# Cross-attention by two levels of Strassen-Winograd products on one core: a fifth product in blocks, left sums by accumulating DMA

## The chip, the cores and the metric

The kernel runs on one core of a Trainium2 chip. The metric is the device time of one execution in microseconds (us); smaller is better. The profile comes from one further execution, with the hardware profiler on.

## What is computed

The reference, for each of 8 batches (C1 = C2 = 512, N = 1024, D = 64, all float32):

```python
q = einsum('bcn,dc->bnd', x1, Wq) + bq
k = einsum('bcn,dc->bdn', x2, Wk) + bk[:, None]
v = einsum('bcn,dc->bdn', x2, Wv) + bv[:, None]
attn = softmax(einsum('bnd,bdm->bnm', q, k), axis=2)
out = einsum('bcm,bnm->bcn', v, attn) + x1
```

The kernel never forms v. It multiplies the raw context by the exponentials first (y = x2 times e, with the contraction over the 1024 context positions m), scales y by the reciprocals of the sums of e, and then multiplies by Wv (o = Wv y), adding bv and x1 at the end.

## The kernel before

**Tiling and stages.** All eight batches run one after the other; `period(s, n, nn, nnn)` (L720) works on batch s and prepares the next ones (n, nn, nnn). The batch index `s.b` counts from 0, so `s.b == 2` is the third batch; the text below calls it batch 3. In a period the matrix engine (PE) runs, in this order:

- products 1, 2 and 6 of y, each a 256 x 512 result in two banks,
- the scores of the next batch for half 0 (the first 512 of the 1024 queries), then its following queries (`queries`, L158),
- products 5, 7 and 3 of y,
- the scores of the next batch for half 1, then keys (`keys`, L169),
- product 4 of y,
- the seven products of o (1, 6, 2, 5, 7, 3, 4).

**The two levels.** y is one 2 x 2 Strassen-Winograd product: left operands are the quarters "11", "12", "21", "22" of x2 transposed (`a`, L128) and their sums S1 to S4 (`left_sums`, L101), right operands are the exponentials `e` and their sums T1 to T4 (`right_sums`, L259). Seven products give four quarters of the result. A product is done either directly (`multiply`, L319: 2 x 4 matmuls of 512 columns) or once more by Strassen-Winograd, "in blocks" (7 x 2 matmuls of 256 columns). In blocks there are two forms. `multiply_seeded` (L415) opens new banks and copies its partial results into them on ScalarE (ACT). `multiply_onto` (L445) adds to open banks and copies partial results to a tile `d` in SBUF. Both run seven small products in the order 1, 7, 6, 2, 5, 4, 3. Small products 1, 6, 5 (and 4 in the seeded form) accumulate in one bank called chain, small product 7 in one called third, and an ACT copy takes each partial result out. A product in blocks needs its own sums, made on VectorE (DVE): `inner_left` (L373, four of 128x256) and `inner_right` (L382, four of 128x512).

Before the change products 1, 2, 3, 4 are in blocks from batch 3 on, product 7 in batches 3 to 6 and in the eighth (`seven`, L725), and products 5 and 6 are direct everywhere. Batch 1 has products 3 and 4 in blocks, batch 2 products 2, 3 and 4.

**Order.** The scheduler is switched off (`tc.manual_schedule()`, L948): each engine runs its instructions in the order in which the code issues them, and waits in place when an operand is not there. A dict of hooks hangs other ACT work between the copies of a product in blocks. The engines are PE, DVE, ACT, GpSimd (POOL, which issues accumulating DMAs and runs the all-reduces over partitions) and SyncE (SP, which issues loads and stores).

**PSUM.** Two banks a0, a1, two banks c0, c1, and a pool `ps_s` of two slots (tag "sc"), which scores, keys, queries, chain and third, and the two halves j of the first product of o (`multiply_o1`, L349) share. A new tile in that pool waits until the last reader of the slot is done.

**Names that the steps use.** `copy_first` (L569, ACT) copies tile 0 of the exponentials of half 0 to a running sum, and `add_tile` (L566, POOL) adds tiles 1 to 3 to it by accumulating DMAs of 512 KB, each of which waits for the landing of the one before. `total` (L223) sums over partitions. `shares` (L232) makes the reciprocals and spreads them over partitions by two small DMAs. `evict_y` (L499) adds a bank and a kept partial result, and scales by the reciprocals (`rden`). `sum_y` (L299) makes T1 to T4 of the second level, that of o. `evict_o` (L513) adds the bias, and adds x1 by an accumulating DMA. `load_x` (L122) issues four loads of 512 KB for the queries or keys of a coming batch, which wait until the last matmul that reads the single x tile is done.

Of the kernel before, what the change touches and what calls it, by code (L numbers as in the profile page):

```python
# [15 lines left out]
def kernel(  # L16
# [47 lines left out]
    nc = tc.nc  # L64
# [36 lines left out]
    def left_sums(a, *ks):  # L101

        for k in ks:
            x, y, op = {
                "S1": ("21", "22", ALU.add),
                "S2": ("11", "S1", ALU.subtract),
                "S3": ("11", "21", ALU.subtract),
                "S4": ("12", "S2", ALU.add),
            }[k]
            nc.vector.tensor_tensor(a["21" if k == "S3" else k], a[x], a[y], op)  # L110
            if k == "S3":
                a["S3"] = a["21"]
# [27 lines left out]

    def project(s, nm, w_sb, bank=None):
# [16 lines left out]
    def queries(s):  # L158

        ps = project(s, "q", wq_sb)  # L160
        s.q = sb.tile([P, N], F32, tag="q", name=f"q_{s.b}", bufs=2)
        for h, r, o in ((0, lo, hi), (1, hi, lo)):
            nc.scalar.activation(
                s.q[r, ts(h, H)], ps[r, :], AF.Identity, bias=bq_sb[r, :]
            )
        for h, r, o in ((0, lo, hi), (1, hi, lo)):
            nc.scalar.dma_start(s.q[o, ts(h, H)], s.q[r, ts(h, H)])
# [131 lines left out]
    def sum_y(s, k):  # L299
        if k == "T1":  # L300
            for n in ("T1", "T2", "T4"):
                s.y[n] = sb.tile([P, 2, H], F32, tag=f"y{n}", name=f"y{n}_{s.b}")
            s.y["T3"] = s.y["12"]
        right_sums(s.y, k)
# [44 lines left out]
    def multiply_o1(s):  # L349
# [16 lines left out]
    RIGHT = (  # L366
        ("T3", "22", "12", ALU.subtract),
        ("T1", "12", "11", ALU.subtract),
        ("T2", "T1", "22", ALU.subtract),
        ("T4", "21", "T2", ALU.add),  # L370
    )

# [9 lines left out]
    def inner_right(s, i, x, *tags):  # L382
# [4 lines left out]
        shape = [P, 4 // len(tags), MH // 2, H // 2]  # L387
        sums = [sb.tile(shape, F32, tag=t, name=f"eI{i}{t}_{s.b}") for t in tags]
        for z, (k, x, y, op) in enumerate(RIGHT):
            v[k] = sums[z // shape[1]][:, z % shape[1]]  # L390
            nc.vector.tensor_tensor(v[k], v[x], v[y], op)
        s.inner[i, "t"] = v
# [16 lines left out]
    def inner_parts(s, i):  # L409

        ks = ("third", "chain") if i in (2, 3) else ("chain", "third")
# [64 lines left out]
    def multiply_4(s):  # L476

        d, complete = multiply_onto(s, 4, "u5" if s.b < B - 1 else "a21", "r")
        complete()
        for j in range(2):  # L480
            u6 = s.tmp[6][:, j, :]
            nc.vector.tensor_tensor(u6, u6, d[:, j, :], ALU.add)

    def multiply_3(s, hooks):

        d, complete = multiply_onto(s, 3, "u1", "r", hooks)

        def evict():
            complete()
            s.y["12"] = y = sb.tile([P, 2, H], F32, tag="y12", name=f"y12_{s.b}")  # L490
            for j in (1, 0):
                nc.vector.tensor_tensor(y[:, j, :], s.bank["a", j], d[:, j, :], ALU.add)

        return evict

# [3 lines left out]
    def evict_y(s, k, steps=(1, 2)):  # L499

        bank, add = RESULT[k]
        rden = s.rden.get(int(k[1]) - 1)
        if 1 in steps:
            s.y[k] = sb.tile([P, 2, H], F32, tag=f"y{k}", name=f"y{k}_{s.b}")
        y = s.y[k]
        for step in steps:
            for j in range(2):
                if step == 1:
                    nc.vector.tensor_tensor(y[:, j, :], s.bank[bank, j], s.tmp[add][:, j, :], ALU.add)  # L509
                else:  # L510
                    nc.vector.tensor_tensor(y[:, j, :], y[:, j, :], rden, ALU.mult)  # L511
# [198 lines left out]
    def scores_and(n, h, bank, project):  # L710


        for i in range(MH):
            scores(n, h, i, bank if i == 2 else None)()
# [5 lines left out]
    def period(s, n, nn, nnn):  # L720

        late = s.b >= 2
        seven = late and (s.b < B - 2 or n is None)  # L725

        def first(i, hook=None):
            multiply(s, "y", i, s.a, s.t, MH, hook=hook)
# [7 lines left out]
        open_t(s)  # L736
        if n is None:
            load_x(s, x1)
        if late:
            complete_1 = multiply_seeded(s, 1, "y11")  # L740
        else:
            first(1)
        if s.b == 0:
            head_second(s, n)
        if late:
            shares(s, 0)
            sum_e(s, "T1", "T2", of=(0,))
            complete_1()
            sum_e(s, "T1", "T2", of=(2,))
            for i in range(1, MH):  # L750
                fold(s, 1, i, "sum", ALU.add)
            total(s, 1)
        else:
            sum_e(s, "T1", "T2")
            total(s, 0)
        if s.b == 0:
            load_a(n, "11")
            first(2)
            evict_y(s, "11", (1,))
            keys(n)  # L760
            load_x(nn, x1)
            sum_t4(s)
            sums(s, 1)
            shares(s, 0)
            sum_e(s, "T3")
        else:
            complete_2 = multiply_seeded(
                s,
                2,
                "y22",  # L770
                {5: lambda: copy_u1(s, 0), 4: lambda: copy_u1(s, 1)} if late else {},
            )
            if late and n:
                sum_t3(s, 0)
                sum_t3(s, 2)
            elif not late:
                sums(s, 1)
            complete_2()
            evict_y(s, "11", (1,))
            if s.b == 1:  # L780
                shares(s, 0)
            sum_t4(s)
            if not late:
                sum_a(s, "S4")
            if not late or n is None:
                sum_e(s, "T3")
        if s.b == 0:
            load_a(n, "21", "22")
        first(6)
        if s.b == 1:  # L790
            inner_right(s, 4, s.t["T4"], "eT2")
            inner_left(s, 3, s.a["S4"], "aI3")
        if seven:
            inner_left(s, 7, s.a["S3"], "yT4")
        if late:
            sum_a(s, "S4")
            inner_left(s, 4, s.a["22"], "a12")
            evict_y(s, "11", (2,))

        def add_exponential(i):  # L800
            exponential(n, 0, i)
            add_tile(n, 0, i)

        def next_queries():
            queries(nn)
# [7 lines left out]
        if n:  # L813
            scores_and(n, 0, "c", next_queries if nn else nothing)
            for i in range(1, MH):
                fold(n, 0, i, "max", ALU.max)
            highest(n, 0)
        if s.b == 0:
            inner_left(s, 4, s.a["22"], "a12")
            inner_right(s, 4, s.t["T4"], "eT2")  # L820
            inner_left(s, 3, s.a["S4"], "aI3")
        shares(s, 1)
        if seven:
            inner_right(s, 7, s.t["T3"], "yT1", "yT2")
            hooks = [{}, {}]
            if n:
                for i in range(MH):
                    lower(n, 0, i)
                hooks = [
                    {  # L830
                        1: lambda: copy_first(n, 0),
                        6: lambda: add_exponential(1),
                        5: lambda: add_exponential(2),
                    },
                    {6: lambda: add_exponential(3)},
                ]
# [146 lines left out]
```

## Time and profile before

| what | value |
|---|---|
| median of 3 runs | 686.92 us (686.87 to 687.68) |
| the profiled execution | 686.51 us |
| its span, first to last instruction | 684.7 us |
| outside the span | 1.8 us |
| PE busy | 677.9 us |
| DVE busy | 617.2 us |
| ACT busy | 303.6 us |
| POOL busy | 211.5 us |
| DMA share of batches 3 to 5 (window 204.20 to 453.10 us) | 0.74 to 0.75 |
| batch 4, first matmul of product 1 to that of batch 5 | 287.05 to 370.11 us |

How to read it: in the list of groups a row gives a line and engine, the operation, the tiles, a shape, a count, then busy time and the mean of one instruction, then the idle time of the engine ahead of them and what ended it. PE's matmuls appear twice per call (a float32 matmul of the code is two records), so a product of 8 matmuls is a row of 16. In a timeline a row is a run of equal instructions with its start and length; a number in brackets is the time that the engine sat idle before it, and after the arrow is what it waited for. "Issue to landing" of a DMA runs from the start of the issuing instruction to the completion that a waiter sees.

### The profile page before, as it was taken

Reading aid. Unit: us, or ns where it says so; the run is one execution under the profiler, and the core shown is the slowest. Engines: PE = TensorE matmul, PEld = TensorE weight load, DVE = VectorE, ACT = ScalarE, POOL = GpSimd, SP = SyncE. Lnnn points to the kernel's source line nnn. Section 1 sums busy time; section 2 is a strip of 40 time slices with the busy share of each in tenths; the row PEclk is TensorE's granted clock in tenths of the full one; section 3 lists DMA queues with packets and bytes.
Section 4 is the critical chain, followed back from the end, with each engine's and each line's share of the span. In section 5 each row is a group of like instructions: output and inputs, shape, how many; then the busy total and the mean of one; then the engine's idle time right before and its main releaser. Section 6 shows DMA issues by size and latency. Waiting matters only on the chain.

```text
span 684.7 us, 6896 instructions
## 1 busy us (share of the span) xinstructions
PE 677.9 (99%) x2324; PEld 378.3 (55%) x2324; DVE 617.2 (90%) x796; ACT 303.6 (44%) x500; POOL 211.5 (31%) x157
## 2 busy tenths in 40 slices
PE   9999999999999999999999999999999999999997
PEld 5333554535547465565656556464754745556763
DVE  1999998987999997999979998999989979999984
ACT  2734264236345552555524655426545355343220
POOL 0124112521333314243232512734227251424100
PEclk9999999999999999999999999999999999999999
DMA  9666365945747977569677696597942993368403
GB/s 304 264 220 222 81 232 103 219 124 137 246 86 176 188 181 245 102 159 219 177 219 149 138 258 137 194 178 159 247 91 81 224 188 71 70 116 232 114 9 114
DMA packets 46163, 114.28 MB, mean 167 GB/s; under 512 B 5041, under 2 KB 7345, under 8 KB 46129
## 3 DMA queue, kind: packets, MB, share of 16 engines
q0 software_dynamic: 18864, 41.50, 34.9%
q1 hardware_dynamic: 25856, 70.13, 29.5%
q10 hardware_dynamic: 1408, 2.23, 1.1%
q8 instruction: 18, 0.29, 0.2%
q14 instruction: 17, 0.13, 0.1%
HBM read 72.62 MB, written 16.81 MB: 131 GB/s over the span
## 4 chain that ended last, share of the span: by engine, by line
PE 94%; DMA 4%; SPq 1%; ACT 1%; DVE 1%; issue 0%; DVEq 0%
PE ps_ya L334 18%; PE ps_oa L334 12%; PE ps_oc L334 8%; PE ps_yc L398 8%; PE ps_s L191 6%; PE ps_ya L398 5%; PE ps_o L334 4%; PE ps_o L354 4%; PE ps_q L149 4%; PE ps_k L149 3%; PE ps_i4chain L398 3%; PE ps_i3chain L398 3%; PE ps_yc L334 3%; PE ps_i2chain L398 3%; PE ps_i1chain L398 2%; PE ps_i7chain L398 2%
## 5 line engine op out<-in xcount | busy, mean ns | idle before, releaser
L334 PE MATMUL ps_ya<-eT,aS 128*128 128x512 f32 x256 | 113.1, 595 | 0.0
L226 POOL PARTITION_ALL_REDUCE den<-sum x16 | 72.6, 4536 | 58.0 <-DVE sum L215 53.2
L334 PEld LDWEIGHTS ps_ya<-eT,aS 128*128 128x128 f32 x256 | 48.0, 190 | 60.9 <-issue 58.7
L253 ACT ACTIVATE e<-e 128x1024 f32<-128x1024 f32 x60 | 62.5, 1061 | 26.6 <-DVE e L249 25.6
L249 DVE TENSOR_TENSOR e<-e,top 128x1024 f32<-128x1024 f32 x60 | 69.3, 1214 | 3.7 <-POOL top L221 3.7
L221 POOL PARTITION_ALL_REDUCE top<-max x16 | 32.7, 2042 | 108.1 <-DVE max L215 54.7
L334 PE MATMUL ps_oa<-yT,w_S 128*128 128x512 f32 x128 | 57.6, 593 | 0.0
L200 ACT COPY e<-ps_s 128x1024 f32<-128x1024 f32 x46 | 45.7, 1027 | 19.1 <-PE ps_s L191 18.6
L345 ACT COPY uy<-ps_ya 128x512 f32<-128x512 f32 x36 | 21.0, 587 | 64.9 <-PE ps_ya L334 60.2
L191 PE MATMUL ps_s<-q,k 64*128 64x512 f32 x188 | 47.3, 608 | 0.8 <-ACT q L602 0.8
L567 POOL DMA_DIRECT2D sum<-e x21 | 25.8, 1228 | 66.3 <-DMA sum<-e 41.5
L334 PEld LDWEIGHTS ps_oa<-yT,w_S 128*128 128x128 f32 x128 | 24.2, 190 | 30.8 <-issue 29.7
L511 DVE TENSOR_TENSOR y<-y,den 128x512 f32<-128x512 f32 x64 | 40.3, 682 | 0.0
L211 DVE TENSOR_TENSOR max<-max,e 128x1024 f32<-128x1024 f32 x30 | 36.7, 1225 | 3.4 <-DVE max L211 0.5
L238 POOL DMA_DIRECT2D den<-row x16 | 9.0, 560 | 94.6 <-DMA row<-few 94.6
L563 POOL DMA_DIRECT2D uo<-in_x_dram x14 | 16.5, 1180 | 63.1 <-DVE few L234 36.8
L509 DVE TENSOR_TENSOR y<-ps_yc,uy 128x512 f32<-128x512 f32 x48 | 30.7, 679 | 0.0
L345 ACT COPY uo<-ps_oa 128x512 f32<-128x512 f32 x32 | 18.2, 588 | 28.0 <-PE ps_oa L334 28.0
L191 PEld LDWEIGHTS ps_s<-q,k 64*128 64x128 f32 x188 | 16.7, 186 | 24.7 <-issue 18.2
L334 PE MATMUL ps_oa<-y,w_S 128*128 128x512 f32 (+1 forms) x68 | 28.8, 567 | 0.0
L334 PE MATMUL ps_oc<-y,w 128*128 128x512 f32 x64 | 28.8, 592 | 0.0
L334 PE MATMUL ps_o<-y,w 128*128 128x512 f32 x64 | 28.8, 592 | 0.0
(174 smaller groups left out, 1414.6 us busy)
## 6 DMA issues: line engine op xcount, KB each, us to landing
x_in_x_dram<-in_x_dram SPq DMA_DIRECT2D x60, 512.0 KB, 7.7
a<-in_x2T_dram SPq DMA_DIRECT2D x32, 512.0 KB, 7.4
sum<-e POOLq DMA_DIRECT2D x21, 512.0 KB, 5.6
r<-in_x_dram POOLq DMA_DIRECT2D x14, 512.0 KB, 6.9
uo<-in_x_dram POOLq DMA_DIRECT2D x14, 512.0 KB, 7.0
out_dram<-r SPq DMA_DIRECT2D x14, 512.0 KB, 5.2
out_dram<-uo SPq DMA_DIRECT2D x14, 512.0 KB, 4.1
eT<-eT POOLq DMA_DIRECT2D x12, 512.0 KB, 9.4
```

The source lines that it names most:

```text
L149: nc.tensor.matmul(ps[r, :], w_sb[:, c, :], s.x[:, c, ts(h, H)], start=(c == 0), stop=(c == CT - 1),)
L191: nc.tensor.matmul(ps[g], s.k[r, ts(i, P)], s.q[r, ts(h, H)], start=True, stop=True)
L200: nc.scalar.copy(e[:, :, i, :], whole)
L211: nc.vector.tensor_tensor(f, e[:, :, 0, :] if i == 1 else f, e[:, :, i, :], op)
L221: nc.gpsimd.partition_all_reduce(s.top[h], s.mx[h][:, 0, :], P, ReduceOp.max)
L226: nc.gpsimd.partition_all_reduce(s.den[h], s.mx[h][:, 0, :], P, ReduceOp.add)
L249: nc.vector.tensor_tensor(e, e, top, ALU.subtract)
L253: nc.scalar.activation(e, e, AF.Exp)
L334: nc.tensor.matmul(ps[:, n], left[ka][:, k, ts(j, P)], right[kb][:, k, n], start=opens and k == 0, stop=i in (2, 3, 4) and k == n_k - 1, s ...
L345: nc.scalar.copy(s.tmp[i][:, j, :], ps)
L398: nc.tensor.matmul(ps, s.inner[i][ka][:, k, :], s.inner[i, "t"][kb][:, k, :], start=opens and k == 0, stop=z in (2, 3, 4) and k == MH // 2 ...
L511: nc.vector.tensor_tensor(y[:, j, :], y[:, j, :], rden, ALU.mult)
```

## The change

It has five parts. The lines are those of the changed file where the diff shows them.

1. Product 5 of y is in blocks in batches 3 to 6 (`multiply_5`), with `inner_left(s, 5, S1)` and `inner_right(s, 5, T1)` as its sums; product 7 is in blocks in batch 7 too.
2. T3 of the second level is no longer y22 minus y12. Product 3 opens banks of its own (`multiply_seeded(s, 3, "r")`), its left operand S4 changes sign, and `evict_t3` adds product 3 and a copy of product 7 (`copy_7`, ACT). T1, T2 and T4 of the second level are made from y11, y21, y22 and T3.
3. S1, S2 and S3 of batches 3 to 8 come from accumulating DMAs: `begin_s1` loads quarter 21 to the S1 tile (SP), `end_s1` adds quarter 22 (POOL), `negate` writes -S1 to the S2 tile and turns quarter 21 to its negative (ACT, as hooks of product 4, after its small products 6 and 5), and `add_11` adds quarter 11 from DRAM to both (POOL).
4. Fewer and wider DVE instructions: T1 and T3 of `inner_right` in one instruction, one instruction per quarter for the scaling (`scale_y`), one for the sum in `multiply_4`.
5. Another order: in the late periods `copy_first` and the first `add_tile` come after the scores of half 1, `end_s1` after them, then the exponentials and adds of tiles 2 and 3 on both sides of the keys; the inner sums of product 4 and the scaling come after `evict_t3`; the maxima of half 1 after product 4; `total(n, 0)` after product 7 of o; queries go to bank c0.

```diff
+    def begin_s1(s):
+        s.a["S1"] = sb.tile([P, MH, C // 2], F32, tag="aS1", name=f"aS1_{s.b}")
+        nc.sync.dma_start(s.a["S1"], x2T[s.b, 1, 0])
+    def end_s1(s):
+        nc.gpsimd.dma_start(s.a["S1"], x2T[s.b, 1, 1], accum_op=ALU.add)
+    def negate(s, k):
...
+        nc.scalar.mul(s.a[k], s.a["S1" if k == "S2" else "21"], -1.0)
+    def add_11(s, k):
+        nc.gpsimd.dma_start(s.a[k], x2T[s.b, 0, 0], accum_op=ALU.add)
...
+        nc.vector.tensor_tensor(
+            both, part[:, :, :, 1, :], part[:, 0].rearrange("p k r n -> p r k n"), ALU.subtract
+        )
+        nc.vector.tensor_tensor(t2, both[:, 0], v["22"], ALU.subtract)
+        nc.vector.tensor_tensor(t4, v["21"], t2, ALU.add)
...
-        ks = ("third", "chain") if i in (2, 3) else ("chain", "third")
+        ks = ("third", "chain") if i in (2, 7) else ("chain", "third")
...
+    def multiply_5(s):
+        d, complete = multiply_onto(s, 5, "u5", "r")
+        complete()
         for j in range(2):
...
+            nc.vector.tensor_tensor(d[:, j, :], s.bank["a", j], d[:, j, :], ALU.add)
+        s.tmp[5] = d
+    def copy_7(s, j):
+        if j == 0:
+            s.tmp[7] = sb.tile([P, 2, H], F32, tag="u1", name=f"uy7_{s.b}")
+        nc.scalar.copy(s.tmp[7][:, j, :], s.bank["c", j])
+    def evict_t3(s):
+        s.y["T3"] = y = sb.tile([P, 2, H], F32, tag="y12", name=f"yT3_{s.b}")
+        for j in range(2):
+            nc.vector.tensor_tensor(y[:, j, :], s.bank["a", j], s.tmp[7][:, j, :], ALU.add)
...
+            hooks = {7: lambda: copy_7(s, 0), 2: lambda: copy_7(s, 1)}
+            if n:
+                hooks |= {6: lambda: exponential(n, 0, 0), 5: lambda: exponential(n, 0, 1)}
+            complete_3 = multiply_seeded(s, 3, "r", hooks)
+            complete_3()
+            evict_t3(s)
         if n:
             if s.b:
                 load_a(n, "11")
-            scores_and(n, 1, "a", nothing)
+                begin_s1(n)
+            scores_and(n, 1, 2, "a", nothing)
             if s.b == 0:
                 exponential(n, 0, 0)
+            elif late:
+                copy_first(n, 0)
+                add_tile(n, 0, 1)
+                end_s1(n)
+                add_exponential(2)
+            else:
+                end_s1(n)
             if nn:
                 next_keys()
+            if late:
+                add_exponential(3)
+        if late:
+            inner_left(s, 4, s.a["22"], "a12")
+            inner_right(s, 4, s.t["T4"], "eT2")
+            scale_y(s, "11", "T3", "22")
+        sum_y(s, "T2")
         sum_y(s, "T1")
...
-        multiply_4(s)
+        multiply_4(
+            s, {6: lambda: negate(n, "S2"), 5: lambda: negate(n, "S3")} if s.b and n else {}
+        )
+        if s.b and n:
+            add_11(n, "S2")
+            add_11(n, "S3")
```

## The prediction

> **What bounds the kernel now.** I read the page's first part, then PE's waits, then one steady period (batch 4, from 287.05 us) as a timeline engine by engine.
>
> ```profile
> PE 677.9 (99%) x2324; PEld 378.3 (55%) x2324; DVE 617.2 (90%) x796; ACT 303.6 (44%) x500; POOL 211.5 (31%) x157
> ```
>
> ```profile
> PE ps_warm L647 <- DVE warm L644: 1.0, 1, 1.0
> PE ps_s L191 <- ACT q L602: 0.8, 1, 0.8
> PE ps_k L149 <- DMA x_in_x_dram<-in_x_dram: 0.3, 1, 0.3
> PE ps_q L598 <- DMA x_head<-in_x_dram: 0.3, 1, 0.3
> PE ps_ya L334 <- ACT e L244: 0.3, 1, 0.3
> PE ps_i4third L398 <- ACT e L200: 0.3, 1, 0.3
> ```
>
> Columns of the second: who waited for whom, total us, times, longest. PE waits 3 us in all, and after the head only 0.3 us. So the time is PE's list of matmuls: taking matmuls off gains in full, and any stall of PE is lost in full. DVE is the next: 77.7 us of the 83.1 us of batch 4. The question is whether the change makes PE wait. The place where I find one is product 4, on ACT, POOL and SP:
>
> ```profile
> 336.49 1.06 ACT L200 COPY e<-ps_s 128x1024 f32<-128x1024 f32 x1
> 339.88 0.69 ACT L173 ACTIVATE k<-ps_k,bqk_sb 128x512 f32<-128x512 f32 x1 [2.33 <-PE ps_k L149]
> ...
> 342.66 0.37 ACT L407 COPY d<-ps_i4chain 128x256 f32<-128x256 f32 x1 [0.49 <-PE ps_i4chain L398]
> 344.39 0.65 ACT L407 COPY d<-ps_i4chain 128x256 f32<-128x256 f32 x2 [1.35 <-PE ps_i4chain L398]
> ```
>
> ```profile
> 334.46 1.20 POOL L567 DMA_DIRECT2D sum<-e  x1 [5.02 <-DMA sum<-e]
> 340.00 1.17 POOL L567 DMA_DIRECT2D sum<-e  x1 [4.35 <-issue]
> ```
>
> ```profile
> x_in_x_dram<-in_x_dram SPq DMA_DIRECT2D x4, 512.0 KB, 6.5
> sum<-e POOLq DMA_DIRECT2D x1, 512.0 KB, 11.7
> ```
>
> The last fence is the DMA view of 339.5 to 341.5 us; its last column is us from issue to landing. The reader is to see that the accumulating DMA issued at 340.00, together with the four x loads that follow the keys, lands at 351.7, while the one issued alone at 334.46 takes 5.0 us. The DMA view of 341 to 345 us shows packets of the SP queue only: the accumulating DMA moves nothing until the loads are nearly through. The same adds in batches 3 and 5 take 11.1 us (issue 257.49) and 9.1 us (422.12); without x loads (506.00, batch 6) 5.0 us.
>
> **The change part by part.**
>
> *Matmuls off PE.* A direct product takes 6.87 us (ps_ya L334 x16 in the chain), one in blocks 6.04 us (product 1 of batch 4: 286.89 to 292.93). Five products change: product 5 in four batches, product 7 in one. 5 x 0.83 = **-4.15 us**. The program's order agrees: five times 512 columns fewer, nothing else on PE.
>
> *DVE.* For batches 3 to 6, off: S1, S2, S3 (1.21 + 1.23 + 1.22), T3 of the second level (1.22), some 0.6 us by merging pairs of 1.28 us into one of 1.22 us. On: inner sums of product 5 (0.75 + 0.88 for L379, 1.22 + 0.69 + 0.69 for L391) and its completion and two evictions (0.69 + 1.28). Sum +0.7 us. S4 with a scalar factor is not in the trace: between a sum of 1.22 us and twice the 0.743 us of L560, so 1.22 to 1.49; I take 1.3. T1 and T3 in one strided instruction: 1.22 (a plain 128x1024) to 1.28 (the pair). DVE then holds 78.4 us of a period of 82.2 us, and walking its new order against PE's needs I find it ahead at the start of a period: 0 us. It costs the overrun if it doesn't fit (rival C).
>
> *Banks and slots.* Product 3's last chain copy now follows an exponential of 1.06 us on ACT, and `evict_t3` must free a0 before the scores need it; both end within 0.3 us of the need. Bound 0 to 0.4 us per period; I take 0.
>
> *The wait that is added.* `end_s1` is an add of 512 KB that POOL issues behind `add_tile(1)`, which waits for `copy_first`, which ACT runs after the scores of half 1. In batch 4, on the clock of before (the 0.83 us saved moves everything alike): last score copy ends 337.55; copy_first 1.04 -> 338.6; two back-to-back issues stand about 1.05 us apart (L286, x2 in 1.82 us), so S1's add is issued at **339.7**, one add of 512 KB ahead of it, and SP's four x loads at 339.88. ACT reaches `negate(S2)`, which needs that add, after the chain copy of 342.66 to 343.03, the third of product 4. Queued behind it on ACT are the two chain copies now at 344.39, and for their slot waits the second half of the first product of o, at 345.92 + 1.72 = 347.6. From the landing L to that matmul: 1.06 us (L285, the same negation) + 0.65 (the two copies) + some 0.2 for semaphores = 1.9. So PE stalls L + 1.9 - 347.6.
> L from below: the second of the pair of L286 lands 6.8 us after issue, L = 346.5, stall 0.8 us. From above: 11.7 + 3.3 for the add ahead (such pairs land some 3.3 us apart), L = 354.7, stall 9.0 us. I take 13 us, nearest to the three contended rows, of which it has one more add in front: L = 352.7, stall **7.0 us**. Batches 3, 4 and 5 are alike: **+21.0**.
> - Batch 6 has no x loads: issue 505.75, landing 6.8 to 8, take 7.15, L = 512.9, need 513.6: **+1.2** (1.0 to 2.5).
> - Batch 7 has neither loads nor keys: score copies end 583.4, S1's add issued 585.5, L = 592.5 with 7.0 us, plus 1.9, against 588.74 + 1.72: **+3.9** (2.6 to 5.5; the two exponentials ahead of the first chain copy alone hold PE some 2.6).
> - Batch 2: the add stands behind the third sum (issue 170.78), so 171.96, x loads at 174.00. 6.8 to 15 us, take 11: L = 183.0, against 180.04 + 1.72: **+3.1** (0 to 7.1).
>
> S2's and S3's own adds have over 25 us until product 6 and the sums of product 7: hidden.
>
> *Batch 8.* There are no scores between products 3 and 4 there, and the inner sums of product 4 move behind `evict_t3`. After product 3's end DVE does 1.4 (rest of completion, two evictions) + 1.6 (four L379) + 1.2 until T3 is there: 4.2; small product 7 wants it after 0.86: **+3.4** (2.5 to 4). Before, these sums were done at 649.6, ahead of product 4 at 650.74.
>
> *Sum* against the profiled execution: -4.15 + 21.0 + 1.2 + 3.9 + 3.1 + 3.4 = +28.5; span 684.7 + 28.5 = 713.2, plus the 1.8 us outside (686.51 - 684.7) = **715.0 us**. The profiled execution is 0.4 us under the median of 686.92, so the forecast is 4.1% above it. Low end of all terms: -4.15 + 2.4 + 1.0 + 2.6 + 0 + 2.5 = +4.3, 691 us. High end: -4.15 + 27.0 + 2.5 + 5.5 + 7.1 + 4.0 + 0.4 x 5 = +44, 730 us.
>
> [...] The granted clock reads 1.00 in every stretch of this trace, and PE has no gap over 1.0 us, so no run here shows what a gap of 7 us does. [...]
>
> **The rivals.**
>
> A, not slower: *S1 lands in time.* The add of `add_tile(1)` is issued 1.1 us ahead of the loads; if both adds get through before them, L is under 345.7 and the negation hides in product 4. For it: alone an add takes 5.0 us. Against: the add at 422.12, 0.75 us ahead of its loads, still took 9.1, and two in a row 6.8. Left are -4.15 and batch 8's +3.4: **685.8 us**, no change; it needs under 6 us from issue to landing in every batch. With batch 8 hidden as well (DVE ahead there) 682.4, faster.
>
> B, *the queues share evenly*: S1 lands about 9.1 us after issue, stall 3.1 in batches 3 to 5, 0.6 in batch 2: 684.7 + 1.8 - 4.15 + 9.3 + 1.2 + 3.9 + 0.6 + 3.4 = **700.7 us**. For it: the 9.1 us row. Against: 11.1 and 11.7, with nothing in front.
>
> C, *a second wait in the same period.* POOL issues the adds of S2 and S3, and the all-reduce for half 1's maxima, behind `add_tile(3)`, which waits for two landings. Should add 2 land after some 361 us in batch 4, the lowering on DVE and then `inner_right(1)` come late for the next product 1: some 3 us in five batches, **730 us**. DVE overrunning its 82 us would show at the same place and cost as much. Against: 2 us of slack by my walk.
>
> **How the numbers follow.** Forecast (stalls of 4 to 9 us in batches 3 to 5) 0.60; B 0.14; C 0.10; A without change 0.09; A faster 0.07. Predicted 715.0. From 690 to 735 the range leaves out A's two cases and a little beyond C. Under 0.2% is about what a measurement of this kernel can't tell from no change. Faster 0.07, same 0.09, slower 0.84.
>
> **What would show it.** PE's waits name ACT copies (product 4's chain), once per batch from 2 to 7, longest in batches 3 to 5; ACT's wait at the multiplication by -1 names the DMA of S1; its landing is 9 to 15 us; batch 8 has one wait of PE for DVE in product 4. PE's matmul count falls, its list shrinks by 4.15 us. It is wrong if S1's add lands within 6 us, or if PE's waits name DVE first.

## The result and the profile after

The changed kernel takes **727.39 us** (median of 4 runs, 726.58 to 729.57); the kernel before takes 687.09 us beside it. The ratio is 1.059, with a 95% interval of 1.0565 to 1.0615. The forecast was 715.0 us, slower by 4.1%, in a range of 690 to 735. The direction and the place were right. The size was 12.4 us short.

The profiled execution took 727.87 us, with a span of 726.1 us (before 684.7: 41.4 us more) and a mean granted clock of 0.984. First the page's busy times, then PE's waits (who waited for whom; total us, times, longest):

```profile
PE 690.8 (95%) x2384; PEld 396.5 (55%) x2384; DVE 615.4 (85%) x744; ACT 326.6 (45%) x545; POOL 211.5 (29%) x175
```

```profile
PE ps_o L388 <- ACT d L439: 15.4, 5, 5.0
PE ps_i5chain L430 <- ACT d L439: 5.5, 4, 1.7
PE ps_i4third L430 <- DVE eI4eT L419: 3.5, 1, 3.5
PE ps_oa L368 <- ACT uo L379: 2.5, 3, 0.8
PE ps_i4chain L430 <- ACT d L439: 2.0, 1, 2.0
```

Two things are to be seen. PE now waits 28.9 us in these five rows, where before the change it waited 0.3 us after the head (the first 50 us). And PE is *busy* for 690.8 us, though its list of matmuls became 4.15 us shorter: it was 677.9 us and should be 673.8. A wait can't make an engine busier, so something else lengthens the matmuls themselves.

The chain that the prediction describes, in batch 4, on POOL, ACT and PE:

```profile
349.72 1.22 POOL L600 DMA_DIRECT2D sum<-e  x1 [10.59 <-ACT sum L605]
350.45 1.42 POOL L159 DMA_DIRECT2D aS<-in_x2T_dram  x1
```

```profile
354.17 0.37 ACT L439 COPY d<-ps_i4chain 128x256 f32<-128x256 f32 x1 [0.83 <-PE ps_i4chain L430]
362.65 1.06 ACT L167 ACTIVATE aS<-aS 128x1024 f32<-128x1024 f32 x1 [8.10 <-DMA aS<-in_x2T_dram]
363.61 0.63 ACT L439 COPY d<-ps_i4chain 128x256 f32<-128x256 f32 x2
```

```profile
357.43 1.88 PE L388 MATMUL ps_o<-y,w 128*128 128x512 f32 x4
364.29 3.54 PE L388 MATMUL ps_o<-y,w 128*128 128x512 f32 x4 [4.99 <-ACT d L439]
```

S1's add is issued at 350.45 and lands 12.2 us later, as ACT's negation starts at 362.65 after 8.10 us of waiting. The two chain copies stand behind it on ACT, and the second half of o's first product starts 1.64 us after the landing, 4.99 us late. Look also at the duration: four records that take 1.88 us at 357.43 take 3.54 us after the stall. The view by stretches shows why (length, PE, PEld, DVE, ACT and POOL busy, then the granted clock, DMA share and GB/s):

```profile
362.00:364.00 2.00, 0.00 (x0) 0.00 (x0) 0.00 (x0) 1.35 (x3) 0.00 (x0) 1.00 1.10 299
364.00:366.00 2.00, 1.71 (x3) 0.71 (x4) 1.70 (x2) 1.68 (x3) 0.00 (x0) 0.64 1.08 298
366.00:368.00 2.00, 2.00 (x4) 0.93 (x3) 1.86 (x4) 0.09 (x1) 0.00 (x0) 0.50 1.03 400
368.00:370.00 2.00, 2.00 (x6) 0.81 (x5) 1.97 (x2) 0.76 (x2) 1.80 (x3) 1.00 0.92 370
```

Behind the stall the clock falls to half, for 3.41 us (a row that lies partly in such a stretch shows a mean, as 0.64 here). The trace has five of these stretches: 3.41 us in batches 3, 4 and 7, and 6.83 us in batches 5 and 8, 23.9 us in all. Half of that, 11.9 us, is clock that wasn't granted; in 1.4 us of it PE stood still anyway, so PE loses 10.5 us.

### The profile page after: what moved, and what is told of

Same layout as the page of the kernel before. It is cut to its first block, busy times and chain, and to the rows that moved or that the text cites. A ratio compares the mean times of both kernels' runs of the same rounds, so it can differ in the third digit from the quotient of the medians.

```text
span 726.1 us, 7052 instructions
## 1 busy us (share of the span) xinstructions
PE 690.8 (95%) x2384; PEld 396.5 (55%) x2384; DVE 615.4 (85%) x744; ACT 326.6 (45%) x545; POOL 211.5 (29%) x175
## 5 line engine op out<-in xcount | busy, mean ns | idle before, releaser
L368 PE MATMUL ps_ya<-eT,aS 128*128 128x512 f32 x192 | 84.8, 595 | 0.0
L258 POOL PARTITION_ALL_REDUCE den<-sum x16 | 53.3, 3328 | 47.6 <-DVE sum L247 42.6
L368 PEld LDWEIGHTS ps_ya<-eT,aS 128*128 128x128 f32 x192 | 36.1, 190 | 44.5 <-issue 41.9
L368 PE MATMUL ps_oc<-yT,w 128*128 128x512 f32 x128 | 57.4, 592 | 0.0
L388 PE MATMUL ps_o<-y,w 128*128 128x512 f32 x64 | 34.9, 682 | 15.4 <-ACT d L439 15.4
L504 DVE TENSOR_TENSOR d<-d,v 128x512 f32<-128x512 f32 x12 | 8.3, 689 | 42.2 <-ACT d L439 42.2
L379 ACT COPY uy<-ps_ya 128x512 f32<-128x512 f32 x28 | 16.3, 588 | 58.1 <-PE ps_ya L368 48.3
L368 PEld LDWEIGHTS ps_oc<-yT,w 128*128 128x128 f32 x128 | 24.3, 190 | 30.6 <-issue 29.4
L406 DVE TENSOR_TENSOR aI<-a 128x256 f32<-128x256 f32 x54 | 34.3, 676 | 0.0
L223 PEld LDWEIGHTS ps_s<-q,k 64*128 64x128 f32 x188 | 18.0, 186 | 23.9 <-issue 18.1
L388 PEld LDWEIGHTS ps_o<-y,w 128*128 128x128 f32 x64 | 12.9, 211 | 30.8 <-ACT d L439 20.1
```

Source lines behind the costliest of these rows:

```text
L223: nc.tensor.matmul(ps[g], s.k[r, ts(i, P)], s.q[r, ts(h, H)], start=True, stop=True)
L258: nc.gpsimd.partition_all_reduce(s.den[h], s.mx[h][:, 0, :], P, ReduceOp.add)
L368: nc.tensor.matmul(ps[:, n], left[ka][:, k, ts(j, P)], right[kb][:, k, n], start=opens and k == 0, stop=i in (2, 3, 4) and k == n_k - 1, s ...
L388: nc.tensor.matmul(ps, w["11"][:, k, ts(j, P)], s.y["11"][:, k, :], start=k == 0, stop=False, skip_group_check=True)
```

## The experiments

Every run is beside the kernel before (686.8 to 687.1 us); "after" is 727.39 us. The first five move one thing each, or take it back.

**1. S1's add issued early.** Only the place of one issue changes:

```diff
                 begin_s1(n)
+                end_s1(n)
             scores_and(n, 1, 2, "a", nothing)
...
                 add_tile(n, 0, 1)
-                end_s1(n)
                 add_exponential(2)
-            else:
-                end_s1(n)
```

> The changed kernel with one issue moved: POOL adds the second half of S1 right behind the load of the first half, ahead of the scores of half 1 and of the first add of the sum, instead of behind that add. Theory (S1's late landing holds ACT at its negation, ACT holds product 4's chain copies, these hold the second half of o's first product): the wait of ACT for S1 goes from 35.6 us to nearly 0, PE's waits at ps_o for d (15.4 us in 5) go, and with them the stretches at a granted clock of 0.5 to 0.6 behind them (some 1.6 us in each of batches 3 to 5): 727.4 - 15.4 - 4.8 = 707 us. Rival 1 (transfers are what is short, whatever the order): the same bytes pass at the same time, S1 or the add of the first tile is as late as before, or the all-reduce of half 1's maxima, which POOL issues behind the add of the third tile, takes the place of the wait: 712 to 727 us, with waits of PE in product 1 of the next batch. Rival 2 (DVE bounds the changed kernel at 80 us of 91.6): no change, 727 us.

Measured: **706.12 us** (ratio 1.0277, 1.0252 to 1.0303), 21.3 us less than after, clock 0.995. ACT's wait for S1 goes from 35.6 us to 4.3, PE's wait at ps_o from 15.4 to 1.2; both that are left are batch 2's, where POOL issues S1's add behind the three adds of the sum. So the late landing is the main cause, and the transfers as such are not: the same bytes pass. The second rival, DVE as the bound, falls: DVE does its work in a period 5 us shorter. The first rival shows in part. PE's largest single wait for `uo` grows from 0.8 to 1.5 us, and DVE's waits for the all-reduce of half 1's maxima grow from 1.8 us in 1 to this:

```profile
DVE e L281 <- POOL top L253: 8.6, 4, 3.9
```

That is the wait of the prediction's rival C, which the longer stall had covered. Some 1.7 us of the gain (half of 3.41) are chance: batch 7's stall of 2.0 us stands in this run too, but no stretch of low clock follows it (see experiment 6).

**2. The x loads later**, the order on POOL and ACT as in after. `late` holds from batch 3 on, so it is batches 3 to 5 whose loads move (the expectation counts one more):

```diff
             keys(nn)
-            if nnn:
+            if nnn and not late:
                 load_x(nnn, x1)
...
             load_a(nn, "21", "22")
+        if nnn and late:
+            load_x(nnn, x1)
```

> The changed kernel with SP's four x loads for the queries after next issued behind product 4 (in batches 2 to 5), not behind the keys, so that no load runs beside S1's add. The order on POOL and ACT stays. Theory (S1 lands late because the x loads go before it): S1's add lands some 7 to 9 us after its issue instead of 12, ACT's wait for it falls from 8 to 3 to 5 us, PE's stall in batches 3 to 5 from 4.2 to 5.0 us to 0 to 1.5, and no stretch of low clock follows: 727.4 - 11 - 5 = 711 us (707 to 715). Rival 1 (the two adds in a row set the landing, not the loads): stalls stay within 1 us of what they were, 724 to 728 us. Rival 2 (the loads are missed where they now are late): PE waits at the queries for x, over 728 us.

Measured: **712.62 us** (ratio 1.0374, 1.0343 to 1.0406), clock 0.997. In batches 3, 4 and 5 ACT starts the negation 7.4, 8.8 and 7.5 us after S1's issue, in place of 11.5, 12.2 and 11.5. PE's wait at ps_o falls from 15.4 to 4.0 us, 1.5 at most. The loads beside S1's add make 3.4 to 4.1 us of its 12.

**3. S1 to S3 on DVE again** (of batches 3 to 8), blocks and order kept:

```diff
-                begin_s1(n)
...
-                end_s1(n)
...
-        multiply_4(
-            s, {6: lambda: negate(n, "S2"), 5: lambda: negate(n, "S3")} if s.b and n else {}
-        )
-        if s.b and n:
-            add_11(n, "S2")
-            add_11(n, "S3")
+        multiply_4(s)
...
             inner_right(n, 2, n.e[0][:, 1], "eT4")
+            if s.b:
+                sum_a(n, "S1", "S2", "S3")
```

> The changed kernel without its third part: S1, S2 and S3 of batches 2 to 8 are computed on DVE again (three sums of 1.22 us in a period, behind the inner sums of product 2), without the two-step load of S1, the negations on ACT and the adds of S2 and S3. Blocks in product 5, T3 and the order stay. Theory: PE's waits for d at ps_o go, with their low clock, as in the run with S1 early: 707 us if DVE holds 83.6 us of work in a period of some 83; each us by which it doesn't comes back four or five times, so 707 to 713, with PE's first waits naming DVE. Rival (the blocks of product 5 or the new order make the time, not the adds of S1): 722 us or more.

Measured: **705.14 us** (ratio 1.026, 1.0236 to 1.0284). No wait at ps_o is left. The accumulating adds and their negations cost 22 us in the changed kernel (727.39 - 705.14). Taking them out costs nothing on DVE there: batch 4 lasts 85.35 us in this run, of which DVE works 82.46, since the other waits make the period longer than that.

**4. q's copies on SP**, for the 5.5 us that the prediction had not seen; in `queries`:

```diff
-            nc.scalar.dma_start(s.q[o, ts(h, H)], s.q[r, ts(h, H)])
+            nc.sync.dma_start(s.q[o, ts(h, H)], s.q[r, ts(h, H)])
```

> The changed kernel with the two copies of q between partitions issued by SP instead of ACT. Theory for the wait of PE in product 5 (ps_i5chain for d, 5.5 us in 4): its first chain copy on ACT stands behind the two activations of q (1.39 us) and behind ACT's own two issues (2.37 us); without the issues the copy starts about 1.2 to 1.8 us earlier and the wait falls to 0 to 0.5 in each of four batches: 727.4 - 4.5 = 723 us. Rival (the activations of q alone hold the copy, the issues run beside): waits stay at 1.2 to 1.8, 727 us. Rival 2: SP holds its x loads behind q and they land late: more than 728 us.

Measured: **722.00 us** (ratio 1.0505, 1.048 to 1.0531), 5.4 us less than after; the row for ps_i5chain is gone. ACT in batch 4, first of after, then of this run:

```profile
323.15 1.39 ACT L195 ACTIVATE q<-ps_q,bqk_sb 64x512 f32<-64x512 f32 x2 [2.27 <-PE ps_q L181]
323.86 2.37 ACTq L199 DMA_DIRECT2D q<-q  x2
326.35 0.37 ACT L439 COPY d<-ps_i5chain 128x256 f32<-128x256 f32 x1 [1.81 <-issue]
```

```profile
323.38 1.39 ACT L195 ACTIVATE q<-ps_q,bqk_sb 64x512 f32<-64x512 f32 x2 [2.27 <-PE ps_q L181]
324.79 0.37 ACT L439 COPY d<-ps_i5chain 128x256 f32<-128x256 f32 x1
```

Two issues hold ACT from 324.54, where the activations end, to 326.35. Before the change a direct product 5 of 6.87 us, which needs no copy in its midst, lay there. The clock's low stretches differ too (8.5 us not granted in this run for 11.9 in after), and other waits grew by over 1 us, so it is the row for ps_i5chain and ACT's rows that show the cause; that 5.4 us equals its 5.5 is partly chance.

**5. Batch 8's inner sums ahead of T3**, as before:

```diff
             complete_3 = multiply_seeded(s, 3, "r", hooks)
+            if n is None:
+                inner_left(s, 4, s.a["22"], "a12")
+                inner_right(s, 4, s.t["T4"], "eT2")
             complete_3()
             evict_t3(s)
...
         if late:
-            inner_left(s, 4, s.a["22"], "a12")
-            inner_right(s, 4, s.t["T4"], "eT2")
+            if n:
+                inner_left(s, 4, s.a["22"], "a12")
+                inner_right(s, 4, s.t["T4"], "eT2")
             scale_y(s, "11", "T3", "22")
```

> The changed kernel with the inner sums of product 4 put ahead of the completion of product 3 and of the two sums for T3 in the eighth batch alone (the order that the kernel before has there). Theory: PE's wait of 3.45 us for DVE in product 4 goes, and with it the stretch behind it in which four matmuls take 1.9 to 2.05 us instead of 1.03: 727.4 - 3.5 - 3 = 721 us. Rival: the sums end no earlier, since DVE comes late to them from product 7, and the wait moves to product 3's or product 4's next step: 725 to 727 us.

Measured: **723.33 us** (ratio 1.0523, 1.0499 to 1.0547), 4.1 us less than after. The wait of 3.45 us is gone, and batch 8 gets 5.75 us shorter (78.88 to 73.13): 3.45 for the wait and 3.0 for the slow stretch, as reckoned, less a new wait of 0.74 us in product 5. The batches before it are 0.4 us longer together, so the span falls by 5.3 us.

**6. The clock**, tried by filling PE's stalls with matmuls that nobody reads:

```diff
+            whole = ps_s.tile([P, 2, H], F32, tag="sc", name=f"ps_o1{j}_{s.b}")
+            s.bank["p", j] = ps = whole[:, 0, :]
...
+            if j == 0 and s.b in (2, 3, 4):
+                for _ in range(9):
+                    nc.tensor.matmul(
+                        whole[:, 1, :], w["11"][:, 0, ts(0, P)], s.y["11"][:, 0, :], start=True, stop=True, skip_group_check=True
+                    )
```

It stands in `multiply_o1` behind the first half; `s.b` of 2 to 4 are batches 3 to 5.

> The changed kernel with nine matmuls of 128x512 more, whose result nobody reads, between the two halves of o's first product in batches 3, 4 and 5, where PE stands still for 4.2 to 5.0 us; at 0.43 us each they fill 3.9 us of it. Theory (a standstill of over some 3 us lowers the granted clock for about 4 us after it, which costs PE 1.6 us each time): the extra matmuls are hidden in the stall, the granted clock reads 1.00 behind it, and the time falls by 3 x 1.6 to 722.6 us though PE has 11.6 us more to do. Rival 1 (the low clock has another cause, the transfers or the load on the chip): the clock stays as it was and the time too, 727 us. Rival 2 (the matmuls are not hidden, since what PE waits for isn't ACT's copy): up to 739 us.

Measured: **730.98 us** (ratio 1.063, 1.0608 to 1.0652), clock 0.995. The dose was wrong: nine such matmuls took 7.9 us, not 3.9, since one is two records of 0.43 us. They outlast the stall, so the time says little, but the clock reads 1.00 up to batch 8's stall. With five in place of nine:

> As the run with nine extra matmuls, with five: such a matmul of 128x512 in f32 took 0.86 us there (18 records in 7.9 us), twice what was reckoned, so nine outlasted the stall by some 3 us a time; five take 4.3 us and fill the stalls of 4.3, 5.0 and 4.2 us. Theory (the standstill lowers the clock behind it): the granted clock reads 1.00 behind the stalls of batches 3 to 5, and the time falls by 3 x 1.6 less what the extra matmuls overrun by, to 723 us (722 to 725), with 12.9 us more work on PE. Rival (the low clock costs nothing, since PE would be waiting anyway, or has another cause): 727 us or more.

Measured: **725.43 us** (725.32 to 726.02; ratio 1.0565, 1.0552 to 1.0579), 2.0 us less than after with 12.9 us more to do. Batch 4, behind its stall, of which 0.73 us is left:

```profile
363.00:365.00 2.00, 1.89 (x5) 0.94 (x6) 1.88 (x2) 1.50 (x3) 0.00 (x0) 1.00 1.07 304
365.00:367.00 2.00, 2.00 (x6) 0.88 (x5) 1.86 (x4) 0.73 (x2) 0.00 (x0) 1.00 1.03 417
```

So in this kernel the standstill is what lowers the clock: from the first half of o's first product to the second it is 6.91 us for 6.86 in after, the transfers are the same, and only PE is kept at work. The four records of o's second half take 3.40, 3.54 and 3.78 us in batches 3, 4 and 5 of after, 1.98 us in each of them with five extra matmuls. The expectation's "over some 3 us" and "about 4 us" are the author's estimates: the five stretches of after stand behind stalls of 1.98 to 4.99 us, and last 3.41 or 6.83 us. The price in time is less than what PE loses: batches 3, 4 and 5 get shorter by 0.4, 1.1 and 1.5 us, and PE's waits for `uo` rise from 2.5 us in 3 to 4.9 in 6. A part of the slow stretch had covered a wait that comes next.

The trace of after also shows when a stretch comes and how long it is. The five begin at 272.4, 364.6, 453.3, 617.2 and 688.8 us. These lie 27, 26, 48 and 21 times 3.413 us apart ((688.8 - 272.4) / 122), and each stretch is one or two times 3.413 us long. Cut into such steps, batch 5 and the first step of batch 7 read (columns as above):

```profile
449.91:453.33 3.42, 0.53 (x2) 0.00 (x0) 0.00 (x0) 0.29 (x1) 0.00 (x0) 1.00 1.04 296
453.33:456.74 3.41, 2.06 (x3) 1.03 (x4) 1.94 (x3) 2.74 (x5) 0.00 (x0) 0.50 1.08 298
456.74:460.15 3.41, 3.41 (x6) 1.34 (x5) 3.34 (x4) 0.57 (x1) 1.61 (x2) 0.50 1.03 398
```

```profile
613.75:617.16 3.41, 1.43 (x8) 1.08 (x7) 3.41 (x4) 2.46 (x5) 2.17 (x2) 1.00 0.44 76
```

A step in which PE is busy for 0.53 us is followed by half speed; one at half speed with 2.06 of 3.41 us by another; one with 3.41 by full speed. Batch 7's 1.98 us lie within one step, which leaves PE 42% busy (1.43 us), and half speed follows. Over the whole trace of after, the five steps at full speed with PE busy for 0 to 42% are followed by half speed; the next ones, with 46 and 49% (from 357.7 and 323.6 us), are not. Of those at half speed, two with 60 and 72% are followed by another, and five with 85 to 100% by full speed. These are counts from one trace, not a rule. In it a stall of 4.31 us (batch 3) has 3.41 us at half speed behind it, and one of 4.24 us (batch 5) 6.83. So what a stall costs is not read from its length alone, and differences of 2 to 3 us between these runs can come from that, which is an estimate: a step at half speed is 1.7 us of clock. Batch 7's stall, 2.0 us long each time, has no stretch behind it in experiments 1 and 6: in both runs of 6 the second group of four records behind it takes 1.03 us, for 1.67 in after, and the whole run of 1 loses 3.5 us of clock (0.995 of 704.4 us), which batch 8's stretch alone costs in after (half of 6.83).

**7. All repairs of the order.** Experiments 1, 4 and 5 together, and four moves on ACT (a hook's number is the small product that it follows, in the order 1, 7, 6, 2, 5, 4, 3):

```diff
-                hooks |= {6: lambda: exponential(n, 0, 0), 5: lambda: exponential(n, 0, 1)}
+                hooks |= {6: lambda: exponential(n, 0, 0), 4: lambda: exponential(n, 0, 1)}
...
-            if late:
+            if late and nn:
                 add_exponential(3)
...
-            s, {6: lambda: negate(n, "S2"), 5: lambda: negate(n, "S3")} if s.b and n else {}
+            s,
+            ({6: lambda: negate(n, "S2"), 5: lambda: negate(n, "S3")} if late and n else {})
+            | ({3: lambda: [negate(n, "S2"), negate(n, "S3")]} if s.b == 1 else {})
+            | ({4: lambda: add_exponential(3)} if n and not nn else {}),
...
-            exponentials(n, 1, 1)
+            lower(n, 1, 1)
...
         second(5)
+        if s.b and n:
+            exponential(n, 1, 1)
```

> The changed kernel with all its parts and only its order mended: S1 issued early, q copied by SP, the eighth batch's inner sums early, and four moves more on ACT: the second exponential of half 0 behind product 3's last chain copy, that of half 1 behind the copies of product 5 of o, in batch 7 the last exponential of half 0 behind product 4's chain copies, and in batch 2 both negations behind product 4. Theory: PE's waits (28.9 us in all) fall to 3 to 6 us, the clock is 1.00 throughout, and the matmuls taken off show: 686.9 - 4.15 + 0 to 4 = 683 to 687 us. Rival (the all-reduce for half 1's maxima, which POOL issues behind the add of the third tile and the x loads, becomes late once the stalls are gone; or DVE, with 80 us in a period of 82, is late for product 1): 689 to 700 us, with waits of PE in o's products 6 and 5 or in product 1.

Measured: **693.45 us** (691.57 to 695.12; ratio 1.0086, 1.0065 to 1.0108), clock 0.999. The rival came true. POOL in batch 4 of this run, then DVE:

```profile
361.02 1.16 POOL L600 DMA_DIRECT2D sum<-e  x1 [9.50 <-ACT r L589]
361.72 1.38 POOL L171 DMA_DIRECT2D aS<-in_x2T_dram  x1
362.31 1.67 POOL L171 DMA_DIRECT2D a<-in_x2T_dram  x1
362.89 2.85 POOL L253 PARTITION_ALL_REDUCE top<-max  x1
```

```profile
359.90 0.69 DVE L247 TENSOR_TENSOR max<-max 128x512 f32<-128x512 f32 x1
...
365.78 4.63 DVE L281 TENSOR_TENSOR e<-e,top 128x1024 f32<-128x1024 f32 x4 [3.60 <-POOL top L253]
```

The maxima are folded at 360.59, but the all-reduce stands on POOL behind the third tile's add, which is issued at 361.02, once the second add's landing allows it, and behind the adds of S2 and S3. (The view names ACT as the releaser at 361.02; in experiment 1's trace it puts the same issue, at 362.56, down to the landing of the second add, and the run that follows, in which only loads are moved, brings it 6.8 us forward against the batch's start.) With the x loads moved as well, as in experiment 2:

> As the run with all moves, and SP's x loads for the queries after next behind product 4 as well. If the adds beside the loads are what is left late, it is 1 to 4 us faster than that run, 683 to 685 us; if nothing is late there, the same within 1 us; if DVE is the bound, the same.

Measured: **688.05 us** (686.83 to 689.51, 12 runs; ratio 1.0008, 0.9995 to 1.0021). The third add is issued at 351.27, the all-reduce waits for DVE as it should, and DVE's waits for `top` fall from 13.8 to 1.8 us. The loads are worth 5.4 us, more than expected, and the time stays above the expected 683 to 685.

**8. The mended kernel, and two of its parts taken back.** To the run before it adds:

```diff
-        if n is None:
-            load_x(s, x1)
...
             inner_right(s, 3, s.t["22"], "eT1")
+            if n is None:
+                load_x(s, x1)
...
-                add_exponential(2)
+                if nn:
+                    add_exponential(2)
...
-            ({6: lambda: negate(n, "S2"), 5: lambda: negate(n, "S3")} if late and n else {})
-            | ({3: lambda: [negate(n, "S2"), negate(n, "S3")]} if s.b == 1 else {})
-            | ({4: lambda: add_exponential(3)} if n and not nn else {}),
+            ({6: lambda: negate(n, "S2"), 5: lambda: negate(n, "S3")} if late and nn else {})
+            | ({3: lambda: negate(n, "S2")} if s.b == 1 or n and not nn else {})
+            | ({6: lambda: add_exponential(2), 5: lambda: add_exponential(3)} if n and not nn else {}),
...
-            add_11(n, "S3")
+            if late and nn:
+                add_11(n, "S3")
...
         second(1)
+        if s.b == 1 or n and not nn:
+            negate(n, "S3")
+            add_11(n, "S3")
```

> As the run with all moves and later x loads (686.6 us of span, 5.5 us of PE's waits), with three moves more: in batch 7 the last two exponentials of half 0 stand behind the second and the fourth chain copy of product 4 and the negations behind it; in batches 2 and 7 the negation for S3 stands behind the copies of o's first product; in batch 8 the x loads for the result are issued behind product 5, so that they don't delay the write of the result before, whose buffer ACT waits for. Theory: the waits of 1.2, 1.0 and 0.4 us go: 688.0 - 2.6 = 685.4 us, 0.2% faster than before. The full 4.15 us would make it 682.8. Rival: other small waits take their place: 687 to 688 us.

Measured: **686.46 us** (685.12 to 687.75, 12 runs; ratio 0.9988, 0.9977 to 1.0000): 0.1% under before, where 685.4 was reckoned; the interval reaches 1.0000, so it isn't clear of no change. After the head PE waits 0.3 us, as before the change, and its list is the bound again:

```profile
PE 676.2 (99%) x2384; PEld 390.5 (57%) x2384; DVE 616.9 (90%) x744; ACT 326.9 (48%) x545; POOL 211.7 (31%) x175
```

Then the edit of experiment 3 on top of it:

> As the mended kernel, with S1, S2 and S3 on DVE in place of the accumulating DMAs and negations. It tells what that part is worth once nothing stalls. If DVE is then the bound (80 us + 3 x 1.22 = 83.6 us of work in a period of 82.5): 1 to 1.5 us more in each of five periods, 690 to 693 us. If DVE still has room, the same time as the mended kernel or a little less, 683 to 686 us, with fewer bytes moved.

Measured: **692.02 us** (691.41 to 692.81; ratio 1.0076, 1.0063 to 1.0089). With S1 to S3 on DVE, batch 4 grows from 82.73 to 83.89 us, and PE waits 2.7 us in 4 in product 3 (`ps_i3chain <- ACT ps_ya`): the chain copy stands on ACT behind the copy of product 7, which in batch 4 waits 1.02 us for DVE. DVE is late, as the expectation's first case has it. Here the accumulating adds gain 5.6 us; in the changed kernel they cost 22.

And, in the mended kernel, product 5 direct:

```diff
-        five = late and nn is not None
+        five = False
```

> As the mended kernel, with product 5 direct in batches 3 to 6 as before the change (16 matmuls of 0.43 us, 6.87 us, for 6.04 us in blocks; 5.5 us a batch less on DVE). It tells what the blocks are worth: if the reckoning by matmuls holds, 4 x 0.83 = 3.3 us slower than the mended kernel. If the blocks' own waits (first chain copy behind q's activations, the sums on DVE) eat the gain: within 1 us of it or faster.

Measured: **688.30 us** (687.66 to 689.40, 11 runs; ratio 1.0021, 1.0012 to 1.0030): the blocks of product 5 are worth 1.84 us by the medians, not 3.3. From the start of q's matmuls to product 7 it is 9.96 us with blocks (batch 5, 392.52 to 402.48) and 10.55 without (394.24 to 404.79): 0.59 us a batch, 2.4 in batches 3 to 6 of the two traces; between trace and medians the difference isn't explained. The other 0.24 goes at one place: small product 6 starts 0.13 us late (398.06, as ACT's first chain copy, behind q's activations, ends at 398.01), and its four records take 0.10 us more.

The length of some batches, from one start of product 1 to the next, in us:

| kernel | 3 | 4 | 5 | 6 | 7 | 8, to the end |
|---|---|---|---|---|---|---|
| before | 82.82 | 83.06 | 82.99 | 82.81 | 77.02 | 71.93 |
| after | 90.18 | 91.64 | 91.39 | 86.11 | 81.31 | 78.88 |
| S1 early | 84.99 | 86.40 | 84.53 | 84.20 | 78.55 | 78.85 |
| mended | 82.56 | 82.73 | 82.56 | 82.56 | 76.55 | 72.29 |

## Why the prediction was right, and by how much it was off

The direction, the mechanism and the place were right. That the time lies only 12.4 us off (12.9 by the spans) is partly luck: the stalls were taken 11.8 us too large (32.6 for 20.8), and 24.7 us of other costs were not in the sum at all. With the stalls at their measured size the same sum would have given 703 us.

**Matmuls off PE, -4.15 us: right as a count, not in full as time.** Where nothing stalls, blocks give 0.59 us a batch for the reckoned 0.83, and product 4 takes 0.35 us more in the new order (6.49 for 6.14 us in batch 5 of the mended kernel), as its small product 6 waits for ACT's first copies. That leaves 0.25 us, and batches 3 and 6 of the mended kernel are 0.26 and 0.25 us shorter. A row for a product in blocks from one place (product 1) was taken for another, where ACT is busier.

**DVE, 0: right.** S4 with a factor took 1.22 us (1.3 taken), and DVE holds 79.9 us (78.4 reckoned) of batch 4's 91.6. It isn't the bound in the changed kernel. It is close: 3 sums more bind it in the mended one.

**The added wait: right mechanism, sizes too large.** The sums of the prediction's terms, against PE's waits:

| batch | 2 | 3 | 4 | 5 | 6 | 7 | 8 | sum |
|---|---|---|---|---|---|---|---|---|
| predicted | 3.1 | 7.0 | 7.0 | 7.0 | 1.2 | 3.9 | 3.4 | 32.6 |
| measured | 1.27 | 4.31 | 4.99 | 4.24 | 0.59 | 1.98 | 3.45 | 20.8 |

The step "L from above ... I take 13 us" came out at 12.2 in batch 4, 0.8 less. From the landing to PE it was 1.64, not 1.9. No run shows the 0.2 us that stands in it for semaphores: the matmul starts 0.05 us after the end of the two copies (364.24 and 364.29). The need came 8.85 us after the issue, not 7.9: product 4 started 0.5 us behind the issue instead of 0.1, and took 6.49 us instead of 6.13. In batch 7 the wait was, as its last remark put it, at the exponentials ahead of the chain copy (1.98 of "some 2.6"). Batch 8's step was exact. In all, the stalls came nearer to rival B's 18.4 us than to the forecast's 32.6.

The 12.2 us came near the 13 taken, but not as the prediction pictured it. From the trace of the kernel before, it read that the add moves nothing until the loads are nearly through. The add's first packet there goes at 345.4 us, when 1.24 of the loads' 2.1 MB had moved. In the changed kernel the first add goes ahead of the loads: it is issued 1.33 us before them (349.72 and 351.05), where before the loads were issued first, by 0.12 us. The views of 341 to 345 us before and of 351.5 to 354.5 us after each show one queue alone, the loads' and then POOL's:

```profile
q1 hardware_dynamic: 304, 1.11, 89.9%
```

```profile
q0 software_dynamic: 231, 0.47, 111.2%
```

**What was missing, and made up for that and more.** First, the clock, 10.5 us. The forecast's sum left it out: the clock reads 1.00 in each of the eight stretches of the trace before, and the prediction said that no run showed what a gap of 7 us does. In after, the stalls of batches 3, 4 and 7 (4.31, 4.99 and 1.98 us) have 3.41 us at half speed behind them, those of batches 5 and 8 (4.24 and 3.45 us) 6.83 us. Second, two waits on ACT: 5.5 us in product 5, whose first chain copy stands behind ACT's own DMA issues, and 2.5 us at `uo`, where ACT does exponentials of half 1 first. The prediction walked product 4 on ACT, but not product 5, which it moved to a new kind. Third, "Banks and slots ... I take 0": the rows of the last two score tiles of half 1 read 1.37 us for 1.02 in batch 4, so that keys start 0.35 us late; it is part of the 6.2 us of small starts below.

The account in us of span: -4.15 + 20.8 + 8.0 + 10.5 = 35.2, and 6.2 of small starts, which is the remainder and not measured by itself: 41.4. This is a split by the records, not a sum of independent prices, as the run with the five extra matmuls shows.

**Rival A** did not happen (12.2 us, not under 6). Its sum also left out batch 7's "some 2.6", which by the prediction's own remark doesn't depend on S1. **Rival B** (9.1 us for a landing in batches 3 to 5) did not happen either: 11.5, 12.2 and 11.5. Its 0.6 us for batch 2 is 1.2 by its own terms (171.96 + 9.1 + 1.9 - 181.76); 1.27 was measured. **Rival C** named a true mechanism that this kernel hides behind the larger stall; it appears as soon as that is mended. The signs to look for came as written, but for PE's list. Its count of matmul records rose from 2324 to 2384, since a product in blocks is 28 short records for 16 long ones, and they took longer, by the clock and by late starts.

What stays open: what decides whether the adds or the loads move first, and how the sixteen DMA engines share between them. The runs show the order in these two traces and the landing times, not the rule.

## What to carry to other kernels

An engine that works in order passes on a late transfer to everything behind the instruction that needs it (here ACT's wait of 8.10 us for S1 held PE for 4.99 us): put such an instruction behind the copies that others wait for, or issue its transfer ahead of the bulk loads (21.3 us here). Look for a low clock behind a stall of PE (10.5 us here, beside 20.8 us of stalls), and when an order is mended, expect the next wait that it covered. When a step becomes several short ones with copies between, walk the copying engine's queue, its DMA issues among it, at that place.

## What the runs showed of the hardware that was not expected

Two sums on DVE took 3.17 us beside POOL's all-reduce, for 0.75 in the same batch where no all-reduce runs (at 333.54). The mended kernel's batch 4, then the same place with S1 to S3 on DVE:

```profile
302.65 3.19 POOL L258 PARTITION_ALL_REDUCE den<-sum  x1
```

```profile
301.95 3.17 DVE L406 TENSOR_TENSOR aI<-a 128x256 f32<-128x256 f32 x2
```

```profile
305.28 3.23 POOL L258 PARTITION_ALL_REDUCE den<-sum  x1 [2.46 <-DVE sum L247]
```

```profile
305.69 1.28 DVE L544 TENSOR_TENSOR y<-ps_yc,uy 128x512 f32<-128x512 f32 x2
```

The pair that takes 3.17 us has both operands in SBUF. In the second run a pair with one operand in PSUM takes 1.28 us beside the all-reduce, as it does ahead of it in the first (at 300.75). The slow pair comes later in the all-reduce there, and takes less:

```profile
306.89 1.24 DVE L406 TENSOR_TENSOR aI<-a 128x256 f32<-128x256 f32 x2
```

What makes the difference, the operands' places or the time within the all-reduce, no run shows. 18 sums of 1.22 us, put back on DVE, raise its busy time by 11.7 us only (616.9 to 628.6), and not by 22: two rows of L406 alone, of 54 sums each, fall from 645 to 586 ns and from 487 to 425 ns a piece, 6.5 us together. That these sums meet the all-reduce at another place in the shifted order is the author's estimate, from the pairs above.
